# Last scale and shift of 32 feed-forward pieces, done one token stage later by way of device memory

## The chip, the cores and the metric

The kernel runs on one core of one Trainium2 chip. The core's engines are TensorE (PE, with its weight loads shown apart as PEld), VectorE (DVE), ScalarE (ACT), GpSimd (POOL) and SyncE (SP, which here only issues transfers). They run at the same time, each works through its own instructions in order, and they wait for one another by semaphores. The metric is device time in microseconds (us) of one execution; lower is better.

## The reference

The input is `x`, 4 images (batches) of 64 x 64 tokens with 256 channels, float32. Two layers are applied in turn:

```python
# layer 0: attention over all 4096 tokens of a batch, and a residual
f = xt @ Wf + bf;  g = xt @ Wg + bg;  v = xt @ Wh + bh
beta = softmax(einsum('bqd,bkd->bqk', g, f))
x = x + (einsum('bqk,bkd->bqd', beta, v) @ Wo + bo)
# layer 1: triangle attention, 8 heads of 32, i, l, j over 64
q, k, v1, v2 = x @ Wq, x @ Wk, x @ Wv1, x @ Wv2
att = softmax(einsum('bilhd,bljhd->biljh', q, k) / sqrt(32), axis=2)
out = einsum('biljh,bilhd,bljhd->bijhd', att, v1, v2)
h = layer_norm(x + out @ Wo) * ln_agg_g + ln_agg_b
z = relu(h @ W1 + b1) @ W2 + b2 + h
return layer_norm(z) * ln_out_g + ln_out_b
```

The change concerns the last line: the multiplication by `ln_out_g` and the addition of `ln_out_b`, which follow the normalisation itself.

## The kernel before

The batches are worked through one after the other. For each there are two stages, and the end of the second layer of one batch is laid into the second stage of the next batch.

**Token stage** (`layer0`): layer 0 of batch b, and the projections q, k, v1, v2 of layer 1. It runs in 64 steps g, `qb, k = divmod(g, 8)`, one block of 512 queries in eight steps. In a step PE computes scores for the next step and sums the values of this one, ACT takes the exponentials (`e`), DVE adds them up (`esum`). The list `parts` spreads the work that closes the block before over the eight steps: `norm` and `bounds` at k=0, `output` (which writes `yT` and stores it) at k=1, then the projections, each staged in a `st` tile (3 buffers) and stored by SP. The stage's end sets up the next one.

**Triangle stage** (`first_layer1` for batch 0, `next_layer1` for the others): 32 steps of the triangle attention. In a step eight products of attention weights and v2, 128 x 2048 each, are made by DVE (`R`, 3 buffers) or by POOL (`Rp`, 2 buffers); `npool` gives POOL 3 and 2 of the eight in turn in batches 1 to 3. PE then sums each over l (`acc`, line 984), ACT takes the sums out (`ao`), SP stores them. `next_layer1` runs in periods of two steps, in an order written out by hand, `ORDER`: each word is one part of the work, and "/n" sets it back by n periods.

**The feed-forward pieces** (class `Tokens`): the rest of layer 1, in 16 pieces of 256 tokens a batch, one a period. The pieces of batches 0, 1 and 2 are worked in the triangle stages of batches 1, 2 and 3, those of batch 3 by themselves at the end (`alone`). The words that matter here: `so` (sums for the normalisation, which takes a tile `z` of the tag `s4`, 2 buffers, 256 KB), `pp` (`polish`, seven small POOL operations), `fo` (the normalisation, ACT, line 1120, into `z`), and `fi`, which is `finish`: two POOL operations (lines 1210 and 1211) and the store to `out` by SP (line 1212).

In the triangle stages of batches 1 and 2, `ahead` also fetches the first layer's data for the next batch: from step 24 on POOL issues transfers for `gT` and `fT` (lines 261 and 267), and SP loads `v` and `yT`.

Within an engine's queue and within SP's, the order of issue is that of the program text (`tc.manual_schedule()`); buffers are given out in turn within a tag.

Of the kernel before, what the change touches and what calls it, by code (L numbers as in the profile page):

```python
# [10 lines left out]
F32 = mybir.dt.float32  # L11
# [7 lines left out]
P = 128  # L19
C = 256  # L20
# [9 lines left out]
NP = T // 256  # L30
# [37 lines left out]
def attention_then_triangle_kernel(  # L68
# [6 lines left out]
    nc = tc.nc  # L75
# [6 lines left out]
    work = ctx.enter_context(tc.tile_pool(name="work", bufs=2))  # L82
    small = ctx.enter_context(tc.tile_pool(name="small", bufs=3))
    dram = ctx.enter_context(tc.tile_pool(name="dram", bufs=2, space=bass.MemoryType.DRAM))
# [83 lines left out]
    def add_b2():  # L168
        b2_bc = work.tile([P, C], F32, tag="st", name="b2_bc", bufs=3)
        nc.gpsimd.dma_start(out=b2_bc, in_=b2.partition_broadcast(P))  # L170
        nc.gpsimd.tensor_tensor(lb2_bc, lb2_bc, b2_bc, ALU.add)
        nc.gpsimd.tensor_tensor(lab2_sb, lab2_sb, lab_sb, ALU.add)
# [19 lines left out]
    def fold_bias():  # L192
        ps = pb("fold")
        for cc in range(2):
            nc.tensor.matmul(ps[:, cc : cc + 1], wo0_sb[:, 0, ts(cc, P)], bh_sb, start=True, stop=True)
        nc.vector.tensor_tensor(bo_sb, bo_sb, ps[:, 0:2], ALU.add)
# [128 lines left out]
    class Ahead:  # L325
# [9 lines left out]
        def load(self, s):  # L335
            if s < self.n:
                self.x = work.tile([P, 4, C], F32, tag="hid", name="xin", bufs=1)
                nc.sync.dma_start(
                    out=self.x, in_=xf[1 + s // 8, ts(s % 8, 512), :].rearrange("(n p) c -> p n c", p=P)
                )  # L340
# [139 lines left out]
    def layer0(b, F, safe, rest, ahead):  # L480
# [13 lines left out]
        def max_piece(qc, t, mx):  # L494
            ps = pb("mxp")
            nc.tensor.matmul(ps, gT[qc // 16][:, ts(qc % 16, P)], fT[t // 4][:, ts(t % 4, 512)], start=True, stop=True)
            nc.vector.tensor_reduce(mx[:, qc % 4, t : t + 1], ps, AX.X, ALU.max)


        def max_row(mx):  # L500
            m = small.tile([P, 4], F32, tag="m", name="m")
            nc.vector.tensor_reduce(m, mx, AX.X, ALU.max)
            ps = pb("row")
            for n in range(4):
                nc.tensor.matmul(
                    ps[:, ts(n, P)], m[:, n : n + 1].to_broadcast([P, P]), ident, start=True, stop=True
                )
            row = work.tile([P, QB], BF16, tag="attP", name="row")
            nc.scalar.mul(row, ps, -1.0)
            return row  # L510

        def pieces(qb):
            mx = small.tile([P, 4, 8], F32, tag="mx", name="mx", bufs=2)
            return mx, [(qb * 4 + n, t) for n in range(4) for t in range(8)]
# [36 lines left out]
        def values(g, ahead):  # L551
            qb, k = divmod(g, 8)
            tt, n = divmod(k, 4)
            if k == 0:
                o_ps[qb] = pc("o")
                esum[qb] = work.tile([P, 4, QB], F32, tag="Rp", name="esum")
            es = e.pop(g)
            for r in range(4):
                if ahead:
                    score(g + 1, r)  # L560
                nc.tensor.matmul(  # L561
                    o_ps[qb], F.v[tt][:, r * 4 + n, :], es[:, r, :],
                    start=(k == 0 and r == 0), stop=(k == 7 and r == 3),
                )
            if k == 0:
                nc.vector.tensor_copy(esum[qb], es)
            else:
                nc.vector.tensor_tensor(esum[qb], esum[qb], es, ALU.add)  # L568
            if k == 7:
                halves = esum[qb]  # L570
                nc.vector.tensor_tensor(halves[:, 0:2], halves[:, 0:2], halves[:, 2:4], ALU.add)
                part = parts_of[qb] = work.tile([P, 2, QB], PART, tag="hid", name="part", bufs=1)
                nc.vector.tensor_tensor(part[:, 0], halves[:, 0], halves[:, 1], ALU.add)
                nc.vector.tensor_tensor(halves[:, 2], halves[:, 0], halves[:, 1], ALU.add)
                nc.vector.tensor_tensor(part[:, 1], halves[:, 2], part[:, 0].bitcast(F32), ALU.subtract)
# [137 lines left out]
        for g in range(8 * NQB):  # L713
            qb, k = divmod(g, 8)
            if b == 0 and not safe:
                for load in later[3 * g : 3 * g + 3]:
                    load()
                if g == 6:
                    fold_bias()
                if g == 20:  # L720
                    add_b2()
            if safe and k == 0 and qb + 1 < NQB:
                mx, todo = pieces(qb + 1)
                for qc, t in todo:
                    max_piece(qc, t, mx)
                row[qb + 1] = max_row(mx)
            values(g, g + 1 < 8 * NQB)

            if qb > 0 and not (qb == last and k >= 6 + late):
                for part in parts[k]:  # L730
                    part(qb - 1)
            if qb == last and k == 3:
                L.fetch_v1(0)
                L.fetch_v1(1)
            if qb == last and k == 5:
                if b > 0:
                    rest.load(NP * (b - 1))
                L.fetch_qk(0, True)
# [272 lines left out]
    class Tokens:  # L1011
        def __init__(self):
            self.ios = []
            self.A, self.htp = {}, {}
            self.h, self.hT, self.hT2, self.hid, self.z, self.zp, self.hps = {}, {}, {}, {}, {}, {}, {}
            self.mv = self.rs = None

        def load(self, tt, far=False):
            b, t = divmod(tt, NP)
# [397 lines left out]
    def next_layer1(b, L, rest, ahead, F):  # L1417
        own = b == NB - 1
# [12 lines left out]
        def load(q, far=False):  # L1431
            if q < NP or 24 + (q - NP) // 2 in stored:
                rest.load(t0 + q, far)
            else:
                held.append((q, far))
# [9 lines left out]
        def moments(q):  # L1445
            if q not in mv:
                mv[q] = small.tile([P, 4, 2], F32, tag="mv", name="mv")
            rest.mv = mv[q]

        def of_piece(word, q):  # L1450
            tt = t0 + q
            first, second = 1 <= q < n1, 0 <= q < n2
            if word in ("h0", "h1"):
                if 2 <= q < n0:
                    n = int(word[1])
                    rest.heads(tt, n, new=q not in mps)
                    mps.setdefault(q, {})["h", n] = True
                    if len(mps[q]) == 2 and q + 1 < n0:
                        load(q + 1)
            elif word == "sa" and first:  # L1460
                moments(q - 1)
                rest.stats(rest.hps[t0 + q], 0)
            elif word == "so" and second:
                moments(q)
                z = rest.z[t0 + q] = work.tile([P, 2, C], F32, tag="s4", name="z")
                rest.sums_of(rest.zp[t0 + q], z, rest.mv, 2)
            elif word == "rr" and second:
                moments(q)
                rest.roots(0 if q + 1 < n1 else 2, 4)
                rs[q] = rest.rs  # L1470
            elif word == "pp" and second:
                moments(q)
                rest.rs = rs.pop(q)
                rest.polish(0 if q + 1 < n1 else 2, 4, nc.gpsimd, back=back_t)
                rn[q] = rest.rn
            elif word == "fa" and first:
                rest.rn = rn[q - 1]
                rest.affine_a(tt)
            elif word == "fo" and second:
                rest.rn = rn[q]  # L1480
                rest.affine_o(tt)
            elif word == "ht" and first:
                rest.turn(tt)
            elif word == "hT" and first:
                rest.normed(tt)
            elif word == "hU" and first:
                rest.carried(tt)
            elif word in ("m0", "m1") and first:
                n = int(word[1])
                mps[q][n] = [rest.hidden(tt, fc) for fc in (2 * n, 2 * n + 1)]  # L1490
            elif word in ("r0", "r1") and first:
                n = int(word[1])
                for fc, mp in zip((2 * n, 2 * n + 1), mps[q][n]):
                    rest.rectify(tt, fc, mp)
            elif word in ("z0", "z1") and second:
                n = int(word[1])
                rest.outputs(tt, n, new=tt not in rest.zp)
                mps.setdefault(q, {})["z", n] = True
            elif word == "fi" and second:
                rest.finish(tt)  # L1500

        def spread(step):
            if F is not None:
# [88 lines left out]
```

## Time and profile before

| | |
|---|---|
| timed runs, median (lowest to highest) | 3689.03 us (3687.88 to 3690.12) |
| the profiled execution, its own time | 3685.46 us |
| its span, first to last instruction | 3683.3 us |
| PE busy | 3562.0 us, 97% |
| DVE busy | 2682.3 us, 73% |
| ACT busy | 1963.3 us, 53% |
| POOL busy | 1763.0 us, 48% |
| line 1210 on POOL | 48 times, 62.2 us |
| line 1211 on POOL | 48 times, 61.9 us |
| moved by DMA | 324.01 MB, mean 88 GB/s |

The page cuts the span into 40 slices and gives each engine's busy share in tenths. For POOL it reads `5000199895999000079999100019999700005999920`: the stretches of 9 are the triangle stages, the zeros between them the token stages. PE shows 9 almost everywhere, DVE 9 in the triangle stages and 4 to 6 in the token stages.

How to read the lines that follow: a group or a row names the source line, the engine, the operation, the tile written and the tiles read, the shape and the count; `[0.48 <-PE acc L984]` says that the engine stood idle for 0.48 us before it and that PE's work on `acc` ended the wait. In a list of waits the three numbers are the sum in us, how many there were, and the longest.

### The profile page before, as it was taken

How to read it: one execution, taken by the hardware profiler on the slowest of the kernel's cores; microseconds unless marked ns; L12 is line 12 of the kernel's file. 1: busy time of each engine (PE TensorE's matmuls, PEld its weight loads, DVE VectorE, ACT ScalarE, POOL GpSimd, SP SyncE). 2: the span in 40 equal slices, each digit the busy share in tenths (PEclk: the TensorE clock that was granted, in tenths of full speed). 3: DMA queues.
4: the chain of work that ended last, by engine and by line, in shares of the span. 5: the costliest groups of instructions: out<-in, count | busy, mean ns of one | idle time of the engine just before them, and what ended most of it. 6: DMA issues, size and time to landing. Idle time of an engine off the chain costs nothing.

```text
span 3683.3 us, 58564 instructions
## 1 busy us (share of the span) xinstructions
PE 3562.0 (97%) x22602; PEld 1930.0 (52%) x22602; DVE 2682.3 (73%) x2142; ACT 1963.3 (53%) x4257; POOL 1763.0 (48%) x918
## 2 busy tenths in 40 slices
PE   9999999988999999999999999999899999999998
PEld 6555444444555555554455555554355555555477
DVE  4555599896555569999555449999755456999976
ACT  3444456554444367665444447676544436677654
POOL 5000199895000079999100019999700005999920
PEclk9999999999999999999999999999999999999999
DMA  9111566566111344425311154333511125431221
GB/s 150 47 46 46 145 160 165 147 160 161 49 52 52 94 117 95 93 50 103 70 54 52 49 142 92 75 91 65 118 43 49 52 74 137 97 91 49 68 65 56
DMA packets 461872, 324.01 MB, mean 88 GB/s; under 512 B 300112, under 2 KB 418640, under 8 KB 452752
## 3 DMA queue, kind: packets, MB, share of 16 engines
q1 hardware_dynamic: 412544, 293.21, 29.9%
q0 software_dynamic: 36160, 19.94, 4.6%
q10 hardware_dynamic: 12880, 7.01, 0.7%
q8 instruction: 181, 2.97, 0.4%
q14 instruction: 107, 0.88, 0.1%
HBM read 176.37 MB, written 143.65 MB: 87 GB/s over the span
## 4 chain that ended last, share of the span: by engine, by line
PE 70%; POOL 7%; issue 3%; DMA 3%; DVE 3%; ACT 2%; SPq 0%; ACTq 0%; POOLq 0%; DVEq 0%
PE acc L984 18%; PE o L561 18%; POOL Rp L974 6%; PE proj L622 6%; PE zp L1196 5%; PE mp L1176 5%; PE s L534 5%; PE hp L1043 3%; PE sp L872 3%; PE v1p L654 2%; DVE R L974 1%; PE y L607 1%; PE att L926 1%; PE hp L1048 1%; PE htp L1143 1%
## 5 line engine op out<-in xcount | busy, mean ns | idle before, releaser
L974 POOL TENSOR_TENSOR Rp<-attP,v 128x2048 f32<-128x2048 f32 x328 | 1491.8, 4576 | 420.0 <-ACT attP L934 370.2
L974 DVE TENSOR_TENSOR R<-att,v 128x2048 f32<-128x2048 f32 x696 | 1548.9, 2274 | 91.0 <-PE acc L984 72.5
L561 PE MATMUL o<-e,v 128*128 128x512 f32 x2048 | 1043.4, 592 | 0.0
L568 DVE TENSOR_TENSOR esum<-esum,e 128x2048 f32<-128x2048 f32 x224 | 512.9, 2290 | 551.7 <-ACT e L546 548.8
L546 ACT ACTIVATE e<-s 128x1024 f32<-128x1024 f32 x512 | 524.0, 1025 | 581.5 <-PE s L534 481.9
L534 PE MATMUL s<-gT,fT 128*128 128x512 f32 x1024 | 785.5, 769 | 8.9 <-ACT e L546 5.1
L984 PE MATMUL acc<-R,wsel 128*32 128x512 f32 x5568 | 698.2, 599 | 16.1 <-DVE R L974 8.1
L1104 POOL TENSOR_SCALAR nt<-mv 128x4 f32<-128x4 f32 (+1 forms) x51 | 9.9, 194 | 1202.9 <-DVE mv L1060 1198.8
L561 PEld LDWEIGHTS o<-e,v 128*128 128x128 f32 x2048 | 388.3, 190 | 276.6 <-issue 233.9
L984 PE MATMUL acc<-Rp,wsel 128*32 128x512 f32 x2624 | 346.6, 600 | 27.2 <-POOL Rp L974 26.5
L994 ACT COPY ao<-acc 128x1024 f32<-128x1024 f32 x256 | 254.8, 1021 | 177.3 <-PE acc L984 166.7
L984 PEld LDWEIGHTS acc<-R,wsel 128*32 128x32 f32 x5568 | 154.7, 109 | 354.5 <-issue 277.3
L534 PEld LDWEIGHTS s<-gT,fT 128*128 128x128 f32 x1024 | 193.9, 190 | 244.4 <-issue 231.4
L909 ACT ACTIVATE es<-S,rd 128x64 f32<-128x64 f32 x1024 | 257.8, 336 | 16.2 <-DVE rd L901 13.4
L1176 PE MATMUL mp<-hT,w 128*128 128x256 f32 x1024 | 249.5, 389 | 0.7 <-ACT hT L1148 0.7
L1196 PE MATMUL zp<-w,hid 128*128 128x256 f32 x1024 | 244.9, 384 | 0.8 <-ACT hid L1185 0.8
L1176 PEld LDWEIGHTS mp<-hT,w 128*128 128x128 f32 x1024 | 186.5, 190 | 101.4 <-ACT hid L1185 36.9
L1196 PEld LDWEIGHTS zp<-w,hid 128*128 128x128 f32 x1024 | 185.5, 190 | 62.5 <-issue 31.9
L584 DVE RECIPROCAL rec<-den 128x512 f32<-128x512 f32 x32 | 107.4, 3357 | 133.6 <-PE den L582 133.6
L984 PEld LDWEIGHTS acc<-Rp,wsel 128*32 128x32 f32 x2624 | 80.2, 110 | 209.1 <-issue 124.8
L1185 ACT ACTIVATE hid<-mp,b_sb 128x256 f32<-128x256 f32 x256 | 105.6, 471 | 117.5 <-PE mp L1176 117.5
L882 ACT ACTIVATE S<-sp 128x512 f32<-128x512 f32 x128 | 129.8, 1116 | 62.9 <-PE sp L872 62.9
(179 smaller groups left out, 3595.1 us busy)
## 6 DMA issues: line engine op xcount, KB each, us to landing
v<-v2d SPq DMA_DIRECT2D x44, 512.0 KB
v1c<-v1d SPq DMA_DIRECT2D x128, 128.0 KB
aT<-ao SPq DMA_DIRECT2D x1024, 16.0 KB
A<-aT SPq DMA_DIRECT2D x256, 64.0 KB
out_dram<-z SPq DMA_DIRECT2D x63, 256.0 KB
y<-yT SPq DMA_DIRECT2D x56, 256.0 KB
q<-st SPq DMA_DIRECT2D x56, 256.0 KB
k<-st SPq DMA_DIRECT2D x52, 256.0 KB
```

The costliest lines, as they stand in the source:

```text
L534: nc.tensor.matmul(s_ps[r // 2][:, r % 2, :], fT[tt][:, ts(r * 4 + n, P)], gT[qb // 4][:, ts(qb % 4, QB)], start=True, stop=not safe,)
L546: nc.scalar.activation(e[g][:, 2 * j : 2 * j + 2, :], s_ps[j], AF.Exp)
L561: nc.tensor.matmul(o_ps[qb], F.v[tt][:, r * 4 + n, :], es[:, r, :], start=(k == 0 and r == 0), stop=(k == 7 and r == 3),)
L568: nc.vector.tensor_tensor(esum[qb], esum[qb], es, ALU.add)
L622: nc.tensor.matmul(ps, w[:, cc, rows], y(qb, cc), start=(cc == 0), stop=(cc == 1))
L882: nc.scalar.activation(self.S[pair][:, :, l0 : l0 + 8].rearrange("p i l -> p l i"), sp[:, lh], AF.Copy if self.safe else AF.Exp,)
L909: nc.scalar.mul(e[:, i, :], rows[:, i, :], rec[:, i : i + 1])
L974: eng.tensor_tensor(R, src.unsqueeze(1).to_broadcast([P, D, N]), v2[h], ALU.mult)
L984: nc.tensor.matmul(acc[32 * c : 32 * c + 32, n % 2, :], w[:, n, c, 16 * h : 16 * h + 32], R[:, ts(c, 8), :].rearrange("p d j -> p (d j)"), ...
L994: nc.scalar.copy(self.ao[step][:, ts(np, 2)].rearrange("p k d j -> p k (d j)"), self.acc[step][np])
L1176: nc.tensor.matmul(self.mp[:, fc % 2, :], w1_sb[:, cc, ts(fc, P)], self.hT[tt][:, cc, :], start=(cc == 0), stop=(cc == 1),)
L1196: nc.tensor.matmul(zp[:, n, :], self.hid[tt][:, fc, ts(n, P)], w2_sb[:, fc, :], start=(fc == 0), stop=(fc == 3 and tt not in self.hT2),)
```

## The change

`finish` is no longer called in the triangle stages of batches 1 and 2. In its place `put_off` stores the normalised `z` as it is to a buffer `raw` in device memory. In the next token stage (batches 2 and 3) `recall` loads a piece back into a tile of the same tag `s4`, in steps g = 0, 3, ... 45, and `finish` is called for it two steps later, in g = 2, 5, ... 47: the two POOL operations and the store to `out`. The pieces of batch 2 (triangle stage of batch 3) and of batch 3 are done as before.

```diff
@@ layer0, the loop over g
             if qb > 0 and not (qb == last and k >= 6 + late):
                 for part in parts[k]:
                     part(qb - 1)
+            if b > 1 and g % 3 == 0 and g < 3 * NP:
+                rest.recall(NP * (b - 2) + g // 3)
+            if b > 1 and g % 3 == 2 and g < 3 * NP:
+                rest.finish(NP * (b - 2) + g // 3)
@@ class Tokens
+            self.raw = {}
+
+        def put_off(self, tt):
+            b, t = divmod(tt, NP)
+            if t == 0:
+                self.raw[b] = dram.tile([NP, P, 2, C], F32, tag="raw", name="raw")
+            nc.sync.dma_start(out=self.raw[b][t], in_=self.z.pop(tt))
+
+        def recall(self, tt):
+            b, t = divmod(tt, NP)
+            self.z[tt] = work.tile([P, 2, C], F32, tag="s4", name="z")
+            nc.sync.dma_start(out=self.z[tt], in_=self.raw[b][t])
@@ next_layer1, of_piece
             elif word == "fi" and second:
-                rest.finish(tt)
+                (rest.finish if own else rest.put_off)(tt)
```

`NP` is 16, and `own` is true for the last batch only.

## The prediction

> **What bounds the kernel now.** I read the chain of waits first: PE holds 70% of it, POOL's Rp products 6%, in one place of each triangle stage. So I cut the stage of batch 1 and the token stage behind it into stretches (microseconds, then busy time of PE, PEld, DVE, ACT, POOL with instruction counts, granted clock, DMA share, GB/s).
>
> ```profile
> 1356.81:1634.46 277.65, 277.65 (x2528) 149.58 (x2524) 268.72 (x191) 196.87 (x541) 266.45 (x141) 1.00 0.34 80
> 1634.46:1764.33 129.87, 116.01 (x837) 52.25 (x828) 119.98 (x77) 74.07 (x213) 126.61 (x79) 0.99 0.41 82
> 2515.50:2645.30 129.80, 117.15 (x836) 52.52 (x824) 119.93 (x77) 74.04 (x213) 126.56 (x79) 0.97 0.42 82
> 1800.00:1850.80 50.80, 50.80 (x144) 26.91 (x143) 30.12 (x22) 21.44 (x24) 0.00 (x0) 1.00 0.14 47
> ```
>
> In the ten even periods (27.77 us each, first row) PE is busy without a gap: nothing taken off POOL can shorten them. In the last 130 us of the stage (second row; third row, the stage of batch 2) PE is idle 13.9 us while POOL is busy 126.6 of 129.9. In the token stage (fourth row) PE is full again and POOL does nothing. So there is one place to win, the tail, and one to lose, the token stage.
>
> POOL's own order of time, in an even period and in the tail (start, duration):
>
> ```profile
> 1400.01 1.30 POOL L1210 TENSOR_TENSOR z<-z,log_bc 128x512 f32<-128x512 f32 x1
> 1401.38 1.29 POOL L1211 TENSOR_TENSOR z<-z,lob_bc 128x512 f32<-128x512 f32 x1
> 1403.16 9.11 POOL L974 TENSOR_TENSOR Rp<-attP,v 128x2048 f32<-128x2048 f32 x2 [0.48 <-PE acc L984]
> ...
> 1679.91 1.29 POOL L1210 TENSOR_TENSOR z<-z,log_bc 128x512 f32<-128x512 f32 x1
> 1681.27 1.28 POOL L1211 TENSOR_TENSOR z<-z,lob_bc 128x512 f32<-128x512 f32 x1
> 1682.51 4.56 POOL L974 TENSOR_TENSOR Rp<-attP,v 128x2048 f32<-128x2048 f32 x1
> 1687.00 1.33 POOL L261 DMA_DIRECT2D gT<-ahgf  x2
> 1688.34 4.56 POOL L974 TENSOR_TENSOR Rp<-attP,v 128x2048 f32<-128x2048 f32 x1
> ```
>
> In the even period the product behind the finish still waits 0.48 us for PE to free an Rp buffer; the finish lies in a wait. In the tail it doesn't: POOL now also issues four transfers a period (2.7 us), and PE has lost its last `sp` group (64 matmuls, 1.98 us, last at 1621.31), so it asks for Rp sooner. POOL's period is 5 x 4.55 + 2.60 (finish) + 1.86 (polish) + 2.70 (issues) = 29.9, which is the measured distance of the polishes (1663.09, 1692.99, 1722.88). Who waits there:
>
> ```profile
> PE acc L984 <- POOL Rp L974: 9.4, 7, 2.7
> ...
> DVE R L974 <- PE acc L984: 8.1, 6, 2.6
> ```
>
> PE waits 9.4 us for POOL, and DVE 8.1 us for PE (it needs its R buffers back).
>
> **What the change removes.** The order of PE's and of DVE's instructions is the same in both programs. From POOL go 32 pieces x (1.296 + 1.290) us, 41 us in each of two triangle stages; 11 of the 16 pieces of a stage cost nothing today (PE's full periods and, at the stage's start, a POOL wait of 2.22 us for PE behind the piece at 1342.77). The last one (1762.38) stands behind the last Rp product. Four in the tail, at 1649.89, 1679.91, 1709.79 and 1739.68, stand ahead of a product. I walk through those, with the durations of the rows and the buffers that each product needs back.
>
> First: the product behind it needs the buffer that PE reads from 1649.95 (0.86 us a product), so it starts at 1650.9, not 1652.5. The one after the issues ends at 1661.4, not 1663.0, and PE, which gets there at 1662.1 and waited 0.78, goes on: 1.0 early, then 1.5 because its 0.54 us for ACT's z, itself behind POOL's polish, goes too. DVE's wait of 0.95 goes; more it can't gain, since it then works without a gap.
> Second: POOL is 4.2 early, no longer last. PE, held to about 1.0 by DVE's R just before, drops its 2.41 wait: 3.4 early. DVE's waits of 0.22 and 2.58 shrink to 0.3 in all: 3.4 early.
> Third: PE's wait of 2.74 goes (6.1 early); DVE drops its 1.70 and is 5.1 early, without a gap.
> Fourth: PE's 0.90 and 1.62 go; DVE, 5.1 early, waits 1.3 of its 2.21 and is 6.0 early; its last 0.30 goes as well: 6.3 us early at the stage's end.
>
> POOL's tail period becomes 27.3 us, DVE's work in an even period is 26.9: what is late next is DVE. The stage of batch 2 has the same waits (PE for POOL 8.8, DVE for PE 8.4), so 6.3 again. Bounds for one stage: no gain at all below; above, DVE's whole idle time in the tail, 129.9 - 120.0 = 9.9, which is near PE's 9.4. I take 6.3, since the walk keeps DVE at its measured work with some of its gaps left.
>
> The store at that place (`fi/2`) stays one 256 KB issue by SP and waits for less (ACT's affine, long done, in place of POOL). It frees the s4 buffer sooner; no engine waits for that buffer in the rows, so nothing.
>
> **What it adds.** In two token stages, 16 times: a 256 KB load by SP, the two POOL operations, a 256 KB store by SP. With the new stores that is 32 x 2 x 0.26 = 17 MB on 324 MB, and 64 more SP issues of about 0.45 us. I cost it at nothing, with this cover. DMA: busy 0.14 in the row above. SP: in program order the load comes after the stores of step g, the store behind those of g+2. The tightest pair after the start (load at g=9, about 1816.9, store at g=11, 1828.3) is 11.4 us apart; the nearest rows for the landing are POOL's transfers of 256 KB, 4.6 and 6.8 us, and one SP load of 256 KB that took 9.56 us in the chain; with 2.7 us of POOL that is 7.3 to 12.3 us, so at worst 0.9 us in which SP's queue stands. Behind it stand the stores of st; ACT's copies into st wait for these, but st has three buffers for the eight stores of 50.8 us. Ends for this: nothing, and 0.9 x 32 = 29 us if each stood on the path; I take nothing. At a token stage's start SP has only v and yT (3 MB, issued at 1771) ahead of the first loads, and its next store only at 1815.9, so three pieces pass unseen.
>
> DVE is the other cover. The tight place comes once in 50.8 us, where `esum` of k=1 follows the reciprocal:
>
> ```profile
> 1812.91 2.28 DVE L568 TENSOR_TENSOR esum<-esum,e 128x2048 f32<-128x2048 f32 x1
> 1815.11 1.40 DVE L608 SCALAR_TENSOR_TENSOR yT<-y,bo_sb,yT 128x512 f32<-128x512 f32 x2
> 1815.29 1.02 ACT L546 ACTIVATE e<-s 128x1024 f32<-128x1024 f32 x1 [3.04 <-DVE esum L568]
> 1818.03 1.88 PE L622 MATMUL proj<-yT,wq 128*128 128x512 f32 x4
> 1819.35 0.80 PE L534 MATMUL s<-gT,fT 128*128 128x512 f32 x1
> ```
>
> ACT's e ends at 1816.31 and its score buffer is wanted at 1819.35: 3.0 us of cover. yT's first half is ready at 1815.8 and wanted at 1818.03: 2.2 us. A POOL piece is 2.6 us. If POOL and DVE don't touch each other, the cost is 0; if a piece holds DVE for its whole length just there, 0.4 us of PE. POOL's products beside DVE's R don't slow it (2274 ns, `esum` beside an idle POOL 2290), so I take 0. But R reads one operand from PSUM, `esum` both from SBUF, and no row has `esum` beside POOL arithmetic.
> The Trainium skill, "SBUF — State Buffer", section "Who interferes with whom", says that a VectorE instruction with two SBUF inputs and a GpSimd instruction that reads SBUF exclude each other, the later one waiting for the end of the earlier. No run here shows it yet; by that rule the sum would come out 3.2 us higher (below).
>
> **The sum.** 2 x 6.3 = 12.6 us less, plus 0. On the profiled execution: 3685.46 - 12.6 = 3672.9 (its span 3683.3 becomes 3670.7; 2.2 lie around it). The median of the timed runs is 3689.03, 3.6 higher than that one, which gives 3676.4.
>
> **The rivals.**
> *DVE takes POOL's place at once* (0.13): it works 26.9 of a period and makes 5.5 of each 8 products, in an order fixed by hand. If only the first two pieces pay, 3.4 a stage: 3689.0 - 6.8 = 3682.2. Against it: DVE's gaps of 1.70 and 2.21 us later in the tail.
> *The whole wait goes* (0.10): PE's 9.4 + 8.8 for POOL: 3670.8. It speaks for it that POOL is the releaser of all of them; against it DVE's 120 us of work.
> *Nothing moves* (0.04): 3689. The products would have to be held by something that the trace puts down to POOL wrongly; but POOL shows no idle time in the tail.
> *Slower* (0.07): POOL's pieces hold DVE in the token stage. Those whose load is issued at k=7 or k=0 can fall on the tight `esum`: g = 0, 15, 24, 39, four a stage, eight in all. With the covers above each costs at most 0.4: 3.2 in all, 3679.6. It decides when the covers are used up before (a backlog of late `esum`s): then 8 x 2.6 = 20.8 against 12.6, 3697. For: no row shows the pair. Against: DVE has 20 us idle of each 50.8, and waits 3.4 us right behind this place.
> This is the skill's rule at its worst.
> That the change doesn't do what it says is out: the 32 pieces stand in the token stages in POOL's order.
>
> **Chances and range.** Forecast 0.66. What this kernel's measurement can tell from no change is about 0.2%, 7.4 us: faster means under 3681.7, slower over 3696.4. The forecast, the whole wait and a little of the first rival are faster: 0.78; the rest of the first, and nothing: 0.15; slower 0.07. The range runs from the whole wait (3670.8) up past the first rival to half of that rival's gain, 3685.5; it leaves out the slower case and nothing moving.
>
> **What would show it.** In the tail POOL shows waits for PE or ACT, the polishes stand about 27.5 us apart instead of 29.9, PE's wait for Rp is under 2 us a stage and DVE's idle time falls by about 6. The even periods stay at 27.77. In the token stage PE stays full, a block stays at 50.8 us, and SP shows no wait for POOL ahead of a store of st. I am wrong if the tail keeps its length with PE waiting for DVE or ACT, or if blocks of the token stage lengthen while `esum` grows over 2.29 us.

## The result, and the profile after

The changed kernel takes 3673.2 us (median of 6 runs, 3671.03 to 3677.77), the kernel before beside it 3689.31 (6 runs, 3686.57 to 3692.3): ratio 0.9959, 95% interval 0.9947 to 0.9971, that is 11 to 20 us less (the two medians lie 16.1 apart). A second measurement (5 runs, under `after_again`) gave 0.9962, 0.9948 to 0.9976. The profiled execution took 3671.03 us with a span of 3668.9; before it was 3685.46 and 3683.3, so 14.4 us less.

First the page's row of POOL's busy tenths in the changed kernel, 40 slices:

```profile
POOL 5000199895000058889312018889721105999920
```

(The page of the kernel before has `5000199895000079999100019999700005999920`; the row printed ahead has three digits too many, a `999` behind its tenth digit.) Where two stretches of 9 stood for the stages of batches 1 and 2, POOL now reads mostly 8, and 1 or 2 in most slices of the token stages behind. The last stage still reads 9.

The stretches that answer to those of before: the even periods of batch 1, the tails of batches 1 and 2, and one block of the token stage (columns as before):

```profile
1357.79:1635.43 277.64, 277.64 (x2528) 149.65 (x2520) 268.70 (x191) 196.53 (x541) 241.00 (x120) 1.00 0.34 80
1635.43:1758.20 122.77, 115.59 (x835) 52.93 (x824) 119.49 (x77) 73.94 (x213) 117.07 (x73) 0.99 0.49 90
2510.40:2633.30 122.90, 114.27 (x837) 52.64 (x825) 119.46 (x77) 73.94 (x213) 117.37 (x73) 1.00 0.47 89
1793.92:1844.72 50.80, 50.80 (x144) 26.91 (x143) 31.89 (x22) 21.42 (x24) 9.23 (x5) 1.00 0.22 73
```

The even stretch lost 25 us of POOL work and is as long as before, 277.64 against 277.65: PE is full in both. Each tail is 7 us shorter, and DVE is now busy 119.5 us of 122.8. In the block of the token stage PE is full as before, with 9.2 us of POOL work in it, and DVE is busy 31.9 us where it was 30.1. So all that can be told apart is in the two tails: 14.1 of the 14.4 us. The stretches outside the tails are up to 2.4 us shorter or 1.7 longer than before, and nearly cancel.

POOL's order of time, at the same two places as before:

```profile
1404.14 9.11 POOL L978 TENSOR_TENSOR Rp<-attP,v 128x2048 f32<-128x2048 f32 x2 [3.09 <-PE acc L988]
...
1673.52 1.36 POOL L261 DMA_DIRECT2D gT<-ahgf  x2
1674.90 9.11 POOL L978 TENSOR_TENSOR Rp<-attP,v 128x2048 f32<-128x2048 f32 x2
1683.94 1.32 POOL L261 DMA_DIRECT2D gT<-ahgf  x2
1685.27 4.58 POOL L978 TENSOR_TENSOR Rp<-attP,v 128x2048 f32<-128x2048 f32 x1
```

In the even period the wait for PE grew from 0.48 to 3.09 us: the 2.6 us taken away became idle time. In the tail two products now follow one another where the finish stood between them.

Who waits in the tail of batch 1 now:

```profile
PE acc L988 <- DVE R L978: 4.4, 6, 2.6
...
DVE R L978 <- PE acc L988: 1.8, 2, 1.4
...
PE acc L988 <- POOL Rp L978: 0.9, 1, 0.9
```

PE's wait for POOL fell from 9.4 to 0.9 us and a wait for DVE of 4.4 took part of its place; DVE's own wait for PE fell from 8.1 to 1.8. What PE waits for in the tail is now mostly DVE.

### The profile page after: what moved, and what is told of

Read it like the earlier page. It is cut to its first block, busy times and chain, and to the rows that moved or that the text cites. A ratio compares the mean times of both kernels' runs of the same rounds, so it can differ in the third digit from the quotient of the medians.

```text
span 3668.9 us, 58713 instructions
## 1 busy us (share of the span) xinstructions
PE 3561.2 (97%) x22602; PEld 1935.0 (53%) x22602; DVE 2700.9 (74%) x2142; ACT 1960.7 (53%) x4257; POOL 1802.8 (49%) x918
## 4 chain that ended last, share of the span: by engine, by line
PE 70%; POOL 6%; issue 4%; DVE 3%; DMA 2%; ACT 2%; SPq 0%; ACTq 0%; POOLq 0%; DVEq 0%
PE o L561 18%; PE acc L988 17%; PE proj L622 6%; PE zp L1213 6%; PE mp L1193 5%; POOL Rp L978 5%; PE s L534 5%; PE hp L1060 3%; PE sp L876 2%; DVE R L978 2%; PE v1p L654 2%; PE y L607 1%; PE att L930 1%; PE hp L1065 1%; PE htp L1160 1%
## 5 line engine op out<-in xcount | busy, mean ns | idle before, releaser
L568 DVE TENSOR_TENSOR esum<-esum,e 128x2048 f32<-128x2048 f32 x224 | 526.1, 2349 | 541.2 <-ACT e L546 538.3
L988 PE MATMUL acc<-Rp,wsel 128*32 128x512 f32 x2624 | 343.9, 596 | 10.8 <-POOL Rp L978 8.5
L1227 POOL TENSOR_TENSOR z<-z,log_bc 128x512 f32<-128x512 f32 x48 | 65.0, 1353 | 454.5 <-DMA z<-raw 435.8
L1213 PEld LDWEIGHTS zp<-w,hid 128*128 128x128 f32 x1024 | 185.6, 190 | 62.4 <-issue 31.9
```

The source lines that it names most:

```text
L988: nc.tensor.matmul(acc[32 * c : 32 * c + 32, n % 2, :], w[:, n, c, 16 * h : 16 * h + 32], R[:, ts(c, 8), :].rearrange("p d j -> p (d j)"), ...
L1213: nc.tensor.matmul(zp[:, n, :], self.hid[tt][:, fc, ts(n, P)], w2_sb[:, fc, :], start=(fc == 0), stop=(fc == 3 and tt not in self.hT2),)
```

## The experiments

Whole executions of one kernel differ by several us, so the runs are also read by stretches of their traces: each tail from the twelfth polish of its stage (1634.46 before, 1635.43 after, in batch 1) to the first score matmul of the next token stage, and each "first block" from there to the first `proj` matmul of k in the second block of 512 queries. All in us, batch 1 / batch 2:

| kernel | ratio to before, 95% interval | tails | first block |
|---|---|---|---|
| before | 1 | 129.87 / 129.89 | 59.77 / 59.77 |
| changed | 0.9959, 0.9947 to 0.9971 | 122.82 / 122.84 | 59.78 / 59.78 |
| e1_four | 0.9968, 0.9958 to 0.9978 | 122.84 / 122.91 | 59.77 / 59.77 |
| e2_twelve | 0.9999, 0.9990 to 1.0009 | 129.68 / 129.73 | 59.78 / 59.76 |
| e3_no_recall | 0.9962, 0.9949 to 0.9976 | 122.77 / 122.84 | 59.80 / 59.79 |
| e4_move_only | 0.9995, 0.9986 to 1.0005 | 129.68 / 129.78 | 59.77 / 59.77 |
| e5_issue_sp | 0.9981, 0.9971 to 0.9990 | 121.84 / 121.88 | 64.74 / 64.33 |
| e6_both | 0.9969, 0.9956 to 0.9981 | 121.34 / 121.32 | 60.89 / 62.52 |
| e7_six | 0.9980, 0.9969 to 0.9990 | 122.89 / 122.87 | 62.10 / 62.14 |
| e8_tight | 0.9963, 0.9950 to 0.9975 | 122.83 / 122.91 | 61.07 / 61.07 |
| e9_issue_sp_split | 1.0014, 1.0004 to 1.0023 | 121.80 / 121.79 | 70.02 / 69.86 |
| e10_both_split | 0.9996, 0.9986 to 1.0006 | 121.33 / 121.33 | 66.39 / 66.39 |
| e11_all_sp_split | 0.9960, 0.9946 to 0.9973 | 121.32 / 121.31 | 59.70 / 59.72 |

The theory: POOL bounded the tail, only the pieces whose work stood ahead of a product there pay, and the added work in the token stage is hidden. The rivals: every piece pays; the earlier store pays; the token stage gives part of the gain back; it was not the sum of POOL's work but the place of the finish.

### Which pieces pay

Only pieces 11 to 14 put off, and then only the other twelve:

```diff
+OFF = (11, 12, 13, 14)        # the other run: (*range(11), 15)
-            if b > 1 and g % 3 == 0 and g < 3 * NP:
+            if b > 1 and g % 3 == 0 and g < 3 * NP and g // 3 in OFF:
...
-                (rest.finish if own else rest.put_off)(tt)
+                (rest.finish if own or q not in OFF else rest.put_off)(tt)
```

> Only pieces 11 to 14 of batches 0 and 1 are put off, the four whose POOL work stood ahead of an Rp product in the tail. Theory (only these four pay, because POOL bounds the tail and PE bounds the even periods): all of the gain, ratio 0.996, about 3674 us against 3689, PE's waits for Rp in a tail under 2 us. Rival (every piece put off pays alike, through the SP queue or the s4 buffer that comes free sooner): 4 of 16 pieces, 3.6 us less, ratio 0.999.

> The complement: pieces 0 to 10 and 15 are put off, 11 to 14 are finished in the triangle stage as before. Theory: no gain, 3689, ratio 1.000; the tails stay at 129.9 us and the even periods at 27.77, with POOL waiting 3.1 us for PE in each instead of 0.5. Rival (every piece pays alike): 12 of 16, 10.8 us less, ratio 0.997.

The four give the tails of the changed kernel to 0.1 us, the twelve those of the kernel before to 0.2 us. The ratios agree: 0.9968 and 0.9999. In the run with twelve, PE's waits for POOL in the tail of batch 1 are nearly the old ones, 8.5 us beside 9.4:

```profile
PE acc L989 <- POOL Rp L979: 8.5, 7, 2.4
```

(In the tail of batch 2 they are 9.7 beside 8.8.) So 24 of the 32 trips through memory do nothing for the time. That every piece pays alike is out: it would have given 3.6 and 10.8 us.

### What the token stage costs

Two kernels: e3_no_recall leaves the added half out (loads, scale and shift, and the stores to `out` of these pieces); e4_move_only moves the data and leaves the work where it was.

```diff
# e3_no_recall: in layer0
-                rest.recall(NP * (b - 2) + g // 3)
-                rest.finish(NP * (b - 2) + g // 3)
# e4_move_only: in next_layer1 and layer0; scaled() does both operations, then put_off
+                (rest.finish if own else rest.scaled)(tt)
-                rest.finish(NP * (b - 2) + g // 3)
+                rest.hand_out(NP * (b - 2) + g // 3)      # the store to out alone
```

> All 32 pieces are put off and never loaded back: their scale and shift and their store to out are left out. It prices the added part in the token stages. Theory (hidden under DMA, SP and DVE slack): the same time as the changed kernel within 1 us, 3673, blocks of 50.81 us. Rival (the added part costs something that the gain covers, by POOL holding DVE): faster than the changed kernel by 0.4 us a piece on a tight place, 3 us, or more.

> The movement without the shift of POOL's work: both POOL operations stay in the triangle stage, the finished piece goes to raw, is loaded back in the token stage and stored to out from there. Theory (POOL's time in the tail is all that pays): 3689, ratio 1.000. Rival (the store without the wait for POOL, or device memory's layout, is part of the gain): can't show here, since the store waits for POOL again; if the time falls by some us, the layout of raw pays; if it rises, the traffic costs.

Without loads, POOL work and stores in the token stage its first block is 59.80 us, with them 59.78; the six blocks behind it take 305.00 us, with them 304.88 (305.00 in the second measurement). The added half costs nothing. Moving the data alone changes nothing either (0.9995, tails 129.7): neither the layout of `raw` nor the traffic counts. In this run the store still waits for POOL, so it says nothing on the earlier store; but the twelve of e2 have the earlier store and gain nothing, and e5 below shortens the tail with no store moved.

### Whether it is the sum of POOL's work

The kernel before, with other work taken from POOL: the twelve of the sixteen transfers `gT` and `fT` that are issued during a stage's steps go to SP's queue (the new argument of `spread_g` and `spread_f` is the queue).

```diff
...
-                spread_g(F, step - 24, d, half)
+                spread_g(F, step - 24, d, half, nc.sync)
...
-                spread_f(F, r, d, 0)
+                spread_f(F, r, d, 0, nc.sync)
```

> The kernel before, with nothing put off, but the twelve transfers gT and fT of each triangle stage of batches 0, 1 and 2 that are issued during its steps (and not the last four) go from POOL's queue to SP's. It takes 2.7 us a period from POOL in place of the finish's 2.6. Theory (the sum of POOL's work in the tail's period bounds it, whatever its parts are): the tails of batches 1 and 2 shrink by 6 to 7 us each as in the changed kernel, and batch 0's stage may gain some us too: 3674 or less. Rival (the finish matters by its place between two products, or by the store behind it): 3689.

> The changed kernel with the same twelve transfers issued by SP. Theory (in the changed kernel DVE is the bound of the tail, 119.5 of 122.8 us): hardly more than one of the two alone in batches 1 and 2, at most 1.6 us a stage, so 3670 plus what batch 0's stage gives. Rival (POOL still bounds the tail, since it shows no idle time there): another 5 us or more a stage, 3660.

A time of 3674 us had been expected of the first, and 3681.18 were measured. The tails shrink by 8.0 us, more than in the changed kernel, with every finish in its old place: it is the sum of POOL's work that bounds, not the place of the finish. But the time falls by only 0.2% (0.9981), since the token stage's first block takes 4.6 to 5.0 us longer. ACT's exponentials there, e5_issue_sp, and PE behind them:

```profile
1758.12 1.95 ACT L546 ACTIVATE e<-s 128x1024 f32<-128x1024 f32 x2
1766.96 1.94 ACT L546 ACTIVATE e<-s 128x1024 f32<-128x1024 f32 x2 [6.89 <-DMA out_dram<-z]
...
1768.04 0.65 PE L534 MATMUL s<-gT,fT 128*128 128x512 f32 x1 [4.22 <-ACT e L546]
```

The tile `e` of step 1 takes the buffer of the last step's `ao`. SP issues the last two steps' 16 stores of `ao` in 15.4 us, up to 7.3 us after the first score (6.2 in the kernels before and changed); the wait is named for the store to out issued right behind them, in e6_both for the stores of `ao` themselves (1763.46, 4.90 us). Which of the two held it in e5 isn't settled. With both edits the tail is 121.3 us, 1.5 less than in the changed kernel, and the first block 1.1 to 2.7 longer. In the tail of batch 1 PE waits 5.2 us for DVE and none for POOL, and POOL waits 6.2 for PE. So DVE bounds that tail, as expected, and the seam behind it takes the gain back.

### What it takes for the token stage to show

Four more POOL operations a piece, first where the change puts the pieces, then with two pieces around the end of each block:

```diff
+            for _ in range(more):                         # more=4
+                junk = work.tile([P, 2, C], F32, tag="h", name="junk", bufs=1)
+                eng.tensor_tensor(junk, z, z, ALU.mult)
# e8_tight, besides:
+AT = [0, 2] + [g for g in range(56) if g % 8 >= 6]
-            if b > 1 and g % 3 == 0 and g < 3 * NP:
+            if b > 1 and g in AT:
```

> The changed kernel with four more POOL multiplications of the same size (128x512, into an unused tile) ahead of each finish in the token stage: six POOL operations a piece, not two. Theory (PE has 2 to 3 us of cover against DVE delays and DVE 20 us of slack in 50.8): the same as the changed kernel, 3673, blocks at 50.8 us, with longer esum rows. Rival (the cover is almost used up by two operations): blocks lengthen; 32 x 5.2 us of POOL time bounds it at 166 us, and 0.4 us a block would show as 5 us in all.

> As the run with six operations, but 14 of the 16 pieces of a stage are loaded at k=6 and k=7, so that two pieces, 15 us of POOL work, stand around the reciprocal, esum and yT of each block. Theory of the cover: one POOL operation holds one esum for at most 1.3 us, less than the 2.2 us that yT has, so 0 to 0.4 us a block, at most 5 us in all: 3673 to 3678. Rival (holds add up over several esums in a row and reach PE): 2.6 us a block or more, 36 us in all, 3709.

Six operations a piece cost 2.3 us a token stage, all of it in the first block; the later blocks stay at 50.8. With two pieces around every block's end it is 1.3 us, again in the first block alone. Here is the end of the first block in e7_six, DVE and then PE:

```profile
1796.48 1.95 DVE L571 TENSOR_TENSOR esum<-esum 128x1024 f32<-128x1024 f32 x1
1798.46 1.41 DVE L573 TENSOR_TENSOR part<-esum 128x512 fp32r<-128x512 f32 x1
1799.79 1.52 DVE L574 TENSOR_TENSOR esum<-esum 128x512 f32<-128x512 f32 x1
1801.35 1.65 DVE L575 TENSOR_TENSOR part<-esum,part 128x512 fp32r<-128x512 f32 x1
1802.93 2.30 DVE L566 COPY esum<-e 128x2048 f32<-128x2048 f32 x1
1805.14 3.35 DVE L584 RECIPROCAL rec<-den 128x512 f32<-128x512 f32 x1
...
1803.06 0.49 PE L582 MATMUL den<-part,ones_f 128*128 128x512 f32 x1 [0.52 <-DVE part L575]
...
1809.27 1.98 PE L607 MATMUL y<-oT,wo 128*128 128x512 f32 x4 [1.35 <-DVE oT L586]
```

Five DVE sums with both operands in SBUF follow one another: the last full `esum`, which took 2.60 us here in place of 2.29, and the four rows shown, 1.23, 0.69, 0.68 and 0.69 us in the kernel before. Behind them the copy for the next block takes 2.30 us in place of 1.22. All of them lie beside POOL operations, and the delays add up to 4.6 us. DVE's wait of 2.2 us for `den`, which stood between the copy and the reciprocal, is used up by that; the 2.4 us left over are what the block lost (2.3). In e8_tight the same sum is 3.6 us, and the block lost 1.3. Both theories missed the place. In the first block PE has no projections between the last sum and `den`, and the cover is those 2.2 us; in the later blocks it is 5.1 us (DVE's wait there), and that holds even with 15 us of POOL work there. DVE's order of time in the kernel before, at the ends of these two blocks:

```profile
1807.72 3.36 DVE L584 RECIPROCAL rec<-den 128x512 f32<-128x512 f32 x1 [2.21 <-PE den L582]
...
1858.54 3.36 DVE L584 RECIPROCAL rec<-den 128x512 f32<-128x512 f32 x1 [5.10 <-PE den L582]
```

The brackets hold the idle time of DVE ahead of the reciprocal: what the sums before it may lose before anything comes later.

### The seam, and a kernel with both

Half of the last step's stores of `ao` given to POOL's queue:

```diff
-                nc.sync.dma_start(
+                queue = nc.gpsimd if step == NSTEP - 1 and 0 < self.b < NB - 1 and d % 2 else nc.sync
+                queue.dma_start(
# e11_all_sp_split, besides: the last four fT
-                    spread_f(F, r, d["gf"], 1)
+                    spread_f(F, r, d["gf"], 1, nc.sync)
```

> The run with the twelve transfers on SP and nothing put off, and in the stages of batches 1 and 2 half of the eight stores of the last step's ao go from SP's queue to POOL's, which is idle then. Theory (its tails were 8.0 us shorter, but the token stage began late, because the exponentials of step 1 need the buffer of that ao and SP issues its eight stores in 7 us): the first block of a token stage goes from 64.5 back to 60 us, the tails stay at 121.9, so 3673 or less. Rival (the late start has to do with the twelve transfers themselves, gT or fT landing later): first block stays at 64 us, 3680.

> The changed kernel with the twelve transfers on SP and the split stores. Theory: tails of 121.3 us (the changed kernel 122.8) and a first block of 59.8 us, so 1.5 us a stage, 3 us in all, under the changed kernel: 3670, if batch 0's stage doesn't lose. Rival (the last microsecond of the tail is DVE's whatever POOL and SP do, and the traffic costs something): the same as the changed kernel, 3673.

> The run with everything on SP and the split stores, and now the last four fT transfers of a stage go to SP's queue too, ahead of the 3 MB of v and yT. Theory (in the run before they were issued at 1759 to 1762 next to these 3 MB and landed only at 1776, where PE waited 5.1 us): in SP's queue they land first, the wait goes, the first block is 59.8 to 60.5 us with tails of 121.3, so 1 to 3 us under the changed kernel, 3671. Rival (the small rows of fT take their 15 us in any queue): the wait of 5 us stays, 3680.

The expectation of the first two failed, and by what the edit itself did. The exponentials came earlier (in e9 6.3 us after the first score, in e5 9.9), but then PE waited for `fT`, 9.0 us in e9 and 5.1 in e10. In e10_both_split, POOL, SP and PE:

```profile
1759.06 2.61 POOL L267 DMA_DIRECT2D fT<-ahgf  x4
...
1759.81 0.37 SPq L397 DMA_DIRECT2D v<-ahv  x1
1760.23 0.45 SPq L399 DMA_DIRECT2D yT<-ahx  x1
...
1776.28 0.76 PE L534 MATMUL s<-gT,fT 128*128 128x512 f32 x1 [5.09 <-DMA fT<-ahgf]
```

The four transfers of `fT` now stood behind POOL's stores and went out together with the 3 MB of `v` and `yT`. In the changed kernel they are issued at 1755.5 to 1758.4, and `v` only at 1765.2. From issue to landing they took 14.4 us here (median) and 4.6 there. The four stores ahead of them landed in 2.5 us (median), so it was hardly these; that it was the 3 MB is argued from the order of issue, and no run moved the 3 MB alone. Put ahead of them in SP's own queue, the four cost nothing (e11, which changes queue and order at once): tails of 121.3 and a first block of 59.7 us, 1.5 us a stage better than the changed kernel. That is under what whole executions can tell: 3673.76 us beside 3688.07, ratio 0.9960, against 0.9959 and 0.9962 of the changed kernel. So it is the better one by its stretches, and the same by its time.

> The changed kernel once more, on the same chip as the two before it, to set them against it: ratio 0.996 as measured, tails 122.8 us, first block 59.8 us.

It measured 0.9962, tails 122.94 and 122.92, first blocks 59.82 and 59.76.

## Why the prediction was right

It was right in direction, place and cause; one term was too small.

- *The place.* "one place to win, the tail": shown by e1 and e2, and by the even periods of 277.64 us.
- *The term.* The walk gave 6.3 us a stage, measured were 7.05. Its steps for DVE hold: it left DVE two waits of 0.3 and 1.3 us, and the trace has 0.22 and 1.41, the second ahead of this row:

```profile
1741.69 15.51 DVE L978 TENSOR_TENSOR R<-att,v 128x2048 f32<-128x2048 f32 x7 [1.41 <-PE acc L988]
```

For PE one step fails: its wait of 0.90 in the fourth period was to go and stands at 0.87. What the walk left out is that DVE's rows get shorter without gaps: seven R in a row take 15.44 or 15.45 us, where five and two with a gap between took 11.05 and 4.49, and four and three 8.85 and 6.92. DVE's busy time in the tail fell from 119.98 to 119.49. That is 0.5 of the missing 0.75; where the rest lies the rows don't settle. The sum for both stages was 12.6, within the measured 11 to 20, and the profiled execution moved by 14.4, of which the tails are 14.1.

- *What is late next.* DVE, as said: PE waits 4.4 us for R and 0.9 for Rp (forecast: under 2), and DVE's waits fell by 6.3 (forecast: about 6). The polishes that stood 29.9 us apart stand 27.3 to 27.4 apart (forecast: about 27.5).
- *Wrong in the signs.* POOL was to show waits in the tail; ahead of its products it shows one, of 1.2 us. Its 27.3 us a period are as long as what DVE and PE leave, so two engines are at the bound together. That is why e6 and e11, which take 2.7 us more from POOL, still win 1.5 us a stage.
- *Nothing for the added half*: shown by e3. SP did wait for POOL ahead of `out`, 28.1 us in four waits in the first of the two token stages. Three of them (13.5, 6.9 and 7.2) lie at the stage's start, where SP's next store came only 51.6 us after the first score in the kernel before (1815.9 against 1764.3), as the prediction had it; the fourth is 0.4, where the prediction allowed 0.9. Of its two landing times for 256 KB the smaller, 4.6, stands beside a 512 KB transfer in the list of the whole run, where `gT` and `fT` read 5.2 and 6.8; the sum doesn't use it.
- *The whole wait goes*: PE's 18.2 us did not all come back, since PE now waits for DVE, 4.4 and 5.3 us. *DVE at once* and *nothing moves* are out by the tails.
- *The slow rival.* Its mechanism is real and its place was wrong. In the changed kernel, POOL and DVE beside each other:

```profile
1784.01 2.86 DVE L568 TENSOR_TENSOR esum<-esum,e 128x2048 f32<-128x2048 f32 x1 [1.76 <-ACT e L546]
...
1784.80 3.21 POOL L1228 TENSOR_TENSOR z<-z,lob_bc 128x512 f32<-128x512 f32 x1
1792.74 3.38 POOL L1228 TENSOR_TENSOR z<-z,lob_bc 128x512 f32<-128x512 f32 x1
...
1795.03 2.19 DVE L571 TENSOR_TENSOR esum<-esum 128x1024 f32<-128x1024 f32 x1
...
1801.65 3.36 DVE L584 RECIPROCAL rec<-den 128x512 f32<-128x512 f32 x1 [1.25 <-PE den L582]
```

POOL's 1.29 us become 3.21 and 3.38, `esum`'s 2.29 become 2.86 and up to 3.32 elsewhere, and the half sum's 1.23 become 2.19. The rule of the Trainium skill quoted in the prediction ("SBUF — State Buffer", section "Who interferes with whom") is what the trace shows: POOL's row at 1784.80 ends 1.1 us after the `esum` that began before it. The half sum at 1795.03 loses 0.96 us, and DVE's wait for `den` falls by as much, from 2.21 to 1.25: the cover at the end of the first block takes it. The prediction looked at `esum` of k=1 in a full block, where PE lost nothing even in e8; with four more operations a piece (e7) the first block paid 2.3 us.

## What to carry to other kernels

Work taken from an engine pays only in the stretches where that engine ends the wait: here 8 of 32 moved pieces, found by cutting a stage into its even periods and its tail, did all of it. Before moving the rest, ask what the relieved engine's slack turns into; in the even periods it turned into idle time, us for us. And where a stage gets shorter, look at the seam behind it: stores that return a buffer and loads that were early by chance decide next, as e5, e9 and e10 show.

## What the runs showed that was not expected

- Outside the parts that the kernels change, stretches differ between executions: the time to the first Rp product 440.5 to 444.8 us, batch 0's triangle stage 440.7 to 445.0, the start of a triangle stage up to its twelfth polish either about 322.5 or 323.9 to 324.3, in kernels with the same code there (322.58 in e7, 324.22 in the changed kernel). The tails of one design agree to 0.2 us. Changes of under 0.1% can be read from the stretch and not from the total.
- Four transfers of 256 KB, issued within about 1 us of 3 MB of large ones, took 14.4 us (median) to land in e10 and 15.7 in e9; the same four took 4.6 in the changed kernel.
- The rows of DVE's R products overlap a little: each is 2.26 to 2.29 us long, and seven in a row without a wait took 15.44, 2.21 each.
